# Gram matrix of a 1x1 convolution's input, with the matmul array used in two halves of 64 columns

## The chip, the cores and the metric

One core of a Trainium2 chip runs the whole program in one launch. The metric is device microseconds of one execution, the median of several; lower is better. All data are fp32.

## The reference, cut to what matters

Two ResNet-like bottleneck blocks run one after the other over 64 images of 1024 channels and 14 x 14 pixels (12,544 pixels in all). Batch norm takes its mean and variance from the batch itself.

```python
def block(x, w1, b1, g1, be1, w2, b2, g2, be2, w3, b3, g3, be3, residual_scale):
    out = relu(bn(conv(x, w1, b1, 1, 0), g1, be1))      # 1x1, 1024 -> 256
    out = relu(bn(conv(out, w2, b2, 1, 1), g2, be2))    # 3x3, 256 -> 256
    out = bn(conv(out, w3, b3, 1, 0), g3, be3)          # 1x1, 256 -> 1024
    return relu(x + softplus(residual_scale)[0] * out)
```

The last batch norm needs the mean and variance of the third convolution's output before that output is used. The kernel doesn't compute the output for that. With y the 256-channel input of the third convolution, the mean of y and the Gram matrix G = y y^T / 12,544 are enough: the mean of output channel c is w_c . mean(y), and its mean square is w_c^T G w_c.

## The kernel before, in words

The input of the third convolution stays in SBUF as `y_all`, 128 partitions by two slots of 12,544 pixels: channels on partitions, 256 channels as 2 x 128. A block runs through four stages: the first convolution, the second by a Winograd-like scheme (`conv2`), the Gram stage with the statistics that follow from it (`gram`, `conv3_stats`), and the third convolution with the residual. In block 0 the last is interleaved with the first convolution of block 1 (`fused`); in block 1 it writes the result (`final`).

The change lies in `gram` (line 994) and `conv3_stats` (line 1099), which run once in each block.

**Gram.** The matmul sums over partitions, so pixels must lie on partitions, and y has channels there. Each tile `zt` holds 256 transposed pixels: two chunks (`CH`) of 128 pixels on partitions by 256 channels, and a last column of ones that gives the channel sums along with the products. There are 49 such tiles in a block, made in two ways:

- `by_tensor` (line 1035) makes the first seven: four TensorE transposes of 128 x 128 into PSUM, and a copy by VectorE (DVE) into `zt` (line 1046).
- `by_vector` (line 1049) makes the other 42, in seven steps of six tiles. `spread` (line 1024) first copies 1536 pixels of y by 16 DMAs into a buffer `home` (one of two; in block 0 one of them is the space of `ws`), so that partitions are shuffled in groups of 32. Nine of the 16 are issued by SyncE (SP), seven by GpSimd (POOL). Then DVE transposes 32 x 32 squares (line 1052), one instruction for each tile. The transfer of step k + 2 is issued after step k's transposes, since it takes their buffer. Before it, `norm_to` (line 1012) applies the second batch norm and ReLU to the pixels that it needs: an activation on ScalarE (ACT, line 544) and a subtraction on DVE (`less`, line 1010), which centres y.

Six `zt` buffers (`NZT`) go round. The matmuls of a tile stand one tile behind its making in PE's order (`before` in lines 1087 to 1097). For every 128 pixels there are two: the first 128 channels against all 256 and the ones (257 columns, into PSUM bank `cp`), and the second 128 channels against themselves and the ones (129 columns, into bank `ap`). The block below the diagonal is the mirror of the one above and isn't computed. Orders are written out by hand: instructions wrapped in `tc.keep_in_program_order` keep the order of the program on their engine, the Gram matmuls and transposes among them.

```python
matmul(g0, before[:, c, 0:P], before[:, c, :], start=first, stop=last)
matmul(g1, before[:, c, P:M], before[:, c, P:], start=first, stop=last)
```

After the last tile, `combined` (line 1401) lets DVE make sums of weights for the next stage (lines 148 to 151): eight instructions in block 0, four in block 1.

**Statistics.** `conv3_stats` scales both banks into SBUF by 1 / 12,544: `g0` by DVE (line 1106), `g1` by ACT (line 1107). DVE doubles the off-diagonal block (`off`, line 1108), since it stands for its mirror too. The means are the last columns. DVE multiplies the weights `w3` by them (lines 1116 and 1117). PE then multiplies G with the weights, in two halves of 512 output channels and for each half three matmuls of 512 columns: `t0` from `g0`, `t1` from `off` and then `g1` (lines 1123 to 1125). DVE multiplies `t0` and `t1` by the weights and adds them (lines 1128 and 1129). Two rounds of eight small matmuls with ones (lines 1131 and 1133) sum over partitions and give mean and mean square. From these comes the affine of the last batch norm, and the residual starts.

One product of the third convolution (`conv3`, line 986) stands on PE between the Gram matmuls and the statistics (`made`, line 1409), another right behind them (line 1412).

Of the kernel before, what the change touches and what calls it, by code (L numbers as in the profile page):

```python
# [37 lines left out]
FP = mybir.dt.float32  # L38
AF = mybir.ActivationFunctionType
ALU = mybir.AluOpType  # L40

P = 128
N, C, H, W = 64, 1024, 14, 14
HW = H * W
M = 256
CS = C // P
MS = M // P
# [5 lines left out]
NPX = N * HW  # L53
CH = 2
NZT = 6

FIRST, LAST = 7, 0
RUN = 3 * P
# [29 lines left out]
def bottlenecks(ctx: ExitStack, tc: tile.TileContext, x, w1s, w2s, w3s, pars, out):  # L88
    nc = tc.nc
# [76 lines left out]
    def matmul(*args, **kw):  # L166

        tc.keep_in_program_order(nc.tensor.matmul(*args, **kw))  # L168
# [825 lines left out]
    def gram(psum, pool, homes, aff, minus_c, beside):  # L994

        g0, g1 = psum.tile(M + 1, "cp"), psum.tile(P + 1, "ap")
        zts = [pool.tile([P, CH, M + 1], FP, tag=f"zt{i}", name=f"zt{i}") for i in range(NZT)]
        for zt in zts:  # L1000
            nc.gpsimd.memset(zt[:, :, M:], 1.0)
        zts = itertools.cycle(zts)

        head = 3 * CH * P
        start = FIRST * CH * P
        bounds = [0, CH * P, head, head + STEP, *range(2 * GPX, NPX + 1, GPX)]
        pieces = list(zip(bounds, bounds[1:]))

        def less(s, y):
            tc.keep_in_program_order(nc.vector.tensor_scalar(y, y, minus_c[:, s : s + 1], None, ALU.add))  # L1010

        def norm_to(end):

            while pieces and pieces[0][0] < end:
                a, e = pieces.pop(0)
                for s in reversed(range(MS)):
                    y = y_all[:, s, a:e]
                    if a == 0 and s == 1:
                        norm_vector(s, y, aff, minus_c[:, s : s + 1])
                    else:  # L1020
                        norm(s, y, aff)
                        less(s, y)

        def spread(k):

            first = start + k * STEP if k else head
            norm_to(first + STEP)
            x = homes[k % 2][:, : MS * STEP].rearrange("p (s j f) -> p s j f", s=MS, j=4)
            for i, j in itertools.product(range(4), range(4)):
                queue = nc.gpsimd if 4 * i + j in (1, 3, 6, 8, 10, 13, 15) else nc.sync  # L1030
                a = first + i * RUN
                queue.dma_start(out=x[32 * i : 32 * i + 32, :, j], in_=y_all[32 * j : 32 * j + 32, :, a : a + RUN])
            return x.rearrange("p s j f -> p (s j) f")

        def by_tensor(a):
            tp = psum.tile(CH * M)
            for c in range(CH):
                for s in range(MS):
                    tc.keep_in_program_order(
                        nc.tensor.transpose(  # L1040
                            tp[:, (c * MS + s) * P : (c * MS + s + 1) * P],
                            y_all[:, s, a + c * P : a + (c + 1) * P], ident,
                        )
                    )
            zt = next(zts)
            tc.keep_in_program_order(nc.vector.tensor_copy(zt[:, :, :M], tp.rearrange("p (c m) -> p c m", c=CH)))  # L1046
            return zt

        def by_vector(x, i):
            zt = next(zts)  # L1050
            tc.keep_in_program_order(
                nc.vector.transpose(
                    zt[:, :, :M].rearrange("p b (n c) -> p b n c", c=32),
                    x[:, :, i * CH * 32 : (i + 1) * CH * 32].rearrange("p n (b r) -> p b n r", r=32),
                )
            )
            return zt

        def pairs():

            norm_to(head)
            then = {
                1: lambda: ready.append(spread(0)),
                2: partial(norm_to, 2 * GPX),
                4: partial(norm_to, 3 * GPX),
                5: lambda: ready.append(spread(1)),
            }
            for i in range(FIRST):
# [12 lines left out]
            norm_to(NPX)  # L1081
            for i in range(LAST):
                yield by_tensor(NPX - (LAST - i) * CH * P)

        ready = []
        total = NPX // (CH * P)
        before = None
        for k, zt in enumerate(itertools.chain(pairs(), (None,))):
            if before is not None:
                for c in range(CH):  # L1090
                    first, last = k == 1 and c == 0, k == total and c == CH - 1
                    matmul(g0, before[:, c, 0:P], before[:, c, :], start=first, stop=last)
                    matmul(g1, before[:, c, P:M], before[:, c, P:], start=first, stop=last)
            before = zt
            if k in beside:
                beside[k]()
        return g0, g1

    def conv3_stats(psum, one, grams, w3, mv, tags, spare):


        g0p, g1p = grams
        g0 = one.tile([P, M + 1], FP, tag="g0", name="g0")
        g1 = one.tile([P, P + 1], FP, tag="g1", name="g1")
        off = one.tile([P, P], FP, tag="goff", name="goff")
        nc.vector.tensor_scalar(g0, g0p, 1.0 / NPX, None, ALU.mult)
        nc.scalar.activation(g1, g1p, AF.Copy, scale=1.0 / NPX)
        nc.vector.tensor_scalar(off, g0[:, P:M], 2.0, None, ALU.mult)
        means = g0[:, M:], g1[:, P:]
        wide = 64  # L1110
        sums = [psum.tile(CS * wide, tag).rearrange("p (o k) -> p o k", k=wide) for tag in ("ax", "ap")]
        ones = one.tile([P, 1], FP, tag="ones", name="ones")
        nc.vector.memset(ones, 1.0)
        ones = ones[:, :1].to_broadcast([P, wide])
        by_mean, w = spare[:, :C], [w3[:, s].rearrange("p o c -> p (o c)") for s in range(MS)]
        nc.vector.tensor_scalar(by_mean, w[0], means[0], None, ALU.mult)
        nc.vector.scalar_tensor_tensor(by_mean, w[1], means[1], by_mean, ALU.mult, ALU.add)
        half = CS // 2
        q = one.tile([P, MS, C], FP, tag="q", name="q")
        for h in range(2):  # L1120
            cols = slice(h * half, (h + 1) * half)
            t0, t1 = (psum.tile(half * P, tag) for tag in tags[2 * h : 2 * h + 2])
            matmul(t0, g0[:, 0:P], w3[:, 0, cols, :], start=True, stop=True)
            matmul(t1, off, w3[:, 0, cols, :], start=True, stop=False)
            matmul(t1, g1[:, 0:P], w3[:, 1, cols, :], start=False, stop=True)
            qs = [q[:, s, h * half * P : (h + 1) * half * P] for s in range(MS)]
            for s, t in ((0, t0), (1, t1)):
                nc.vector.tensor_mul(qs[s], t, w3[:, s, cols, :].rearrange("p o c -> p (o c)"))
            nc.vector.tensor_add(qs[0], qs[0], qs[1])
        for o in range(CS):  # L1130
            matmul(sums[0][:, o], by_mean[:, o * P : (o + 1) * P], ones, start=True, stop=True)
        for o in range(CS):
            matmul(sums[1][:, o], q[:, 0, o * P : (o + 1) * P], ones, start=True, stop=True)
        nc.vector.tensor_copy(mv[:, :, 0], sums[0][:, :, 0])
        nc.vector.tensor_copy(mv[:, :, 1], sums[1][:, :, 0])
        sq = small.tile([P, CS], FP, tag="sq", name="sq")
        nc.vector.tensor_mul(sq, mv[:, :, 0], mv[:, :, 0])
        nc.vector.tensor_sub(mv[:, :, 1], mv[:, :, 1], sq)
# [232 lines left out]
    for b in range(2):  # L1371
# [95 lines left out]
```

## Time and profile before

| | us |
|---|---|
| median of 3 runs | 1944.43 (1944.18 to 1944.73) |
| the profiled execution's own time | 1944.06 |
| its span in the trace | 1942.3 |
| PE busy in the span | 1918.6 |
| DVE busy | 1544.3 |
| Gram matmuls of block 0, first start to last end | 589.7 to 659.7 |
| Gram matmuls of block 1, first start to last end | 1555.2 to 1624.7 |
| statistics in block 0 up to the second conv3 product | 659.8 to 669.7 |

PE is TensorE's matmuls and PEld its weight loads, which the profile lists as records of their own. Each fp32 matmul of the program leaves two matmul records and two load records. The starts of matmul records are measured; their ends are modelled, so distances between starts are the prices to read. In a timeline row the columns are the start, the time until the group's end, engine, line, operation, the tiles written and read, the shape, the count, and in brackets the idle time before and what ended it. All matmuls come from one helper and carry its line, L168, so the tile names tell them apart: `cp<-zt` and `ap<-zt` are the Gram matmuls.

### The profile page before, as it was taken

What the parts mean: (1) busy time and instruction counts of PE and PEld (TensorE: products, weight loads), DVE (VectorE), ACT (ScalarE), POOL (GpSimd) and SP (SyncE); (2) the same over time, 40 slices, a digit from 0 to 9 for tenths busy, and PEclk for the clock granted to TensorE, in tenths of its full rate; (3) what the DMA queues carried; (4) which work ended last, traced back from release to release, by engine and by line L of the source; (5) the groups of instructions that cost most, each with busy time, mean ns of one, the idle gap of its engine ahead of it and who ended that gap; (6) DMA issues with size and microseconds to landing.
All of it is one profiled execution on the core that took longest, in us unless ns stands there. A gap on an engine that the chain in (4) does not pass through costs nothing.

```text
span 1942.3 us, 27081 instructions
## 1 busy us (share of the span) xinstructions
PE 1918.6 (99%) x9438; PEld 1612.1 (83%) x9438; DVE 1544.3 (80%) x2473; ACT 1046.2 (54%) x2098; POOL 575.1 (30%) x674
## 2 busy tenths in 40 slices
PE   9999999999999999999999999999999999999999
PEld 5555557999997799999999999989999987555555
DVE  5778667999998667776776767689999975888886
ACT  2222214677765055555555555456777651666666
POOL 0111100212105133433333334302121051666664
PEclk9999999999999999999999999999999999999999
DMA  7777634887948634444444444258788486899998
GB/s 291 273 250 263 235 129 157 204 221 202 230 141 207 197 137 187 175 166 166 181 185 167 166 178 180 108 181 209 215 208 225 140 194 233 279 334 335 333 342 300
DMA packets 201849, 413.91 MB, mean 213 GB/s; under 512 B 37809, under 2 KB 178001, under 8 KB 185201
## 3 DMA queue, kind: packets, MB, share of 16 engines
q1 hardware_dynamic: 161728, 324.66, 49.0%
q0 software_dynamic: 34368, 36.45, 9.3%
q10 hardware_dynamic: 5616, 51.06, 6.3%
q8 instruction: 75, 1.23, 0.3%
q14 instruction: 62, 0.50, 0.1%
HBM read 263.75 MB, written 115.34 MB: 195 GB/s over the span
## 4 chain that ended last, share of the span: by engine, by line
PE 92%; DVE 5%; DMA 1%; ACT 1%; issue 1%; SPq 0%; POOL 0%; DVEq 0%; ACTq 0%
PE cy L168 17%; PE ay L168 17%; PE columns L168 13%; PE cp L168 12%; PE ap L168 10%; PE m L168 6%; PE l L168 6%; PE cx L168 5%; PE ax L168 4%; PE ps L168 1%; DMA home<-y 1%; ACT y L544 1%; DVE v L628 0%; DVE sums L622 0%; DVE steps L697 0%
## 5 line engine op out<-in xcount | busy, mean ns | idle before, releaser
L331 ACT ACTIVATE cu<-cy,scale 128x196 f32<-128x196 f32 (+1 forms) x552 | 256.7, 474 | 277.5 <-PE cy L168 271.3
L168 PE MATMUL columns<-v,ub 128*128 128x224 f32 (+1 forms) x1536 | 300.7, 337 | 0.0
L331 ACT ACTIVATE x<-x,shift 128x392 f32<-128x392 f32 x428 | 241.1, 613 | 59.5 <-POOL x L490 53.1
L168 PEld LDWEIGHTS columns<-v,ub 128*128 128x128 f32 x1536 | 269.2, 188 | 2.8
L464 DVE SCALAR_TENSOR_TENSOR x<-cp,scale,x 128x196 f32<-128x196 f32 (+1 forms) x368 | 178.2, 484 | 97.2 <-PE cp L168 96.1
L168 PE MATMUL cy<-ct,ws 128*128 128x196 f32 (+1 forms) x736 | 221.9, 383 | 1.1 <-ACT cu L331 1.1
L485 POOL TENSOR_TENSOR x<-x,cu 128x196 f32<-128x196 f32 (+1 forms) x184 | 159.3, 866 | 172.1 <-ACT cu L331 162.5
L168 PE MATMUL ay<-at,ws 128*128 128x196 f32 (+1 forms) x752 | 209.1, 381 | 0.0
L490 POOL TENSOR_TENSOR x<-x,cu 128x392 f32<-128x392 f32 x124 | 125.9, 1016 | 192.8 <-DVE x L464 188.1
L168 PEld LDWEIGHTS ay<-at,ws 128*128 128x128 f32 x752 | 136.5, 190 | 33.4
L168 PEld LDWEIGHTS cy<-ct,ws 128*128 128x128 f32 x736 | 133.3, 190 | 36.4 <-ACT cu L331 4.2
L168 PE MATMUL l<-diffs,ub 128*128 128x224 f32 (+1 forms) x768 | 149.1, 337 | 2.6 <-PE columns L168 2.6
L511 POOL TENSOR_TENSOR x<-x,cu 128x392 f32<-128x392 f32 x120 | 121.9, 1017 | 85.9 <-DVE x L464 62.4
L168 PE MATMUL m<-sums,ua 128*128 128x224 f32 (+1 forms) x752 | 145.9, 337 | 1.5 <-DVE sums L622 1.5
L168 PEld LDWEIGHTS l<-diffs,ub 128*128 128x128 f32 x768 | 134.3, 189 | 4.4 <-PE columns L168 3.9
L331 ACT ACTIVATE au<-ay 128x196 f32<-128x196 f32 (+1 forms) x141 | 53.8, 381 | 155.2 <-PE ay L168 152.4
L464 DVE SCALAR_TENSOR_TENSOR x<-cx,scale,x 128x196 f32<-128x196 f32 (+1 forms) x184 | 89.1, 484 | 57.4 <-PE cx L168 57.4
L168 PEld LDWEIGHTS m<-sums,ua 128*128 128x128 f32 x752 | 131.3, 189 | 3.3 <-DVE sums L622 2.9
L168 PE MATMUL cx<-y,w 128*128 128x196 f32 (+1 forms) x404 | 124.1, 392 | 0.4 <-DVE x L1148 0.4
L168 PE MATMUL cy<-y,w 128*128 128x196 f32 (+1 forms) x404 | 123.8, 392 | 0.0
L168 PE MATMUL cp<-zt 128*128 128x257 f32 x392 | 118.0, 382 | 1.8 <-DVE zt L1046 1.7
L168 PE MATMUL cp<-y,ws 128*128 128x196 f32 (+1 forms) x368 | 113.6, 390 | 0.9 <-DVE x L464 0.9
(216 smaller groups left out, 3924.8 us busy)
## 6 DMA issues: line engine op xcount, KB each, us to landing
x<-in_x SPq DMA_DIRECT2D x62, 1568.0 KB, 6.8
ub<-u SPq DMA_DIRECT2D x94, 768.0 KB, 5.2
x<-mid SPq DMA_DIRECT2D x32, 1568.0 KB, 8.2
mid<-x ACTq DMA_DIRECT2D x31, 1568.0 KB, 5.1
out<-x SPq DMA_DIRECT2D x123, 392.0 KB, 5.7
ua<-u SPq DMA_DIRECT2D x94, 256.0 KB, 3.0
u<-y POOLq DMA_DIRECT2D x48, 256.0 KB, 5.8
home<-y SPq DMA_DIRECT2D x90, 96.0 KB, 4.3
```

The costliest lines, as they stand in the source:

```text
L168: tc.keep_in_program_order(nc.tensor.matmul(*args, **kw))
L331: tc.keep_in_program_order(nc.scalar.activation(*args, **kw))
L464: nc.vector.scalar_tensor_tensor(v, bank, self.scale[:, o : o + 1], v, ALU.mult, ALU.add)
L485: nc.gpsimd.tensor_add(self.part(1, 1), self.part(1, 1), u3)
L490: nc.gpsimd.tensor_add(v, v, self.u12)
L511: nc.gpsimd.tensor_add(v, v, self.u12[:, i * self.n : (i + 1) * self.n])
L544: act(y, y, AF.Relu, bias=shift[:, s : s + 1], scale=scale[:, s : s + 1])
```

## The change

The 256 channels are cut into four groups of 64 (`Q`). Of the sixteen 64 x 64 blocks of G ten are computed, each pair of groups once. For every 128 pixels there are four matmuls, each with 64 columns of weights and all 128 rows of the array. A `tile_position` puts them alternately in the array's lower and upper 64 columns, so that their results fall on PSUM partitions 0 to 63 and 64 to 127. Group 0 meets groups 0, 1, 2 and a column of ones (193 columns) and group 1 meets 1, 2, 3 and ones (193), both into bank `cp`; group 2 meets 2, 3 and ones (129), and group 3 meets group 0 with one unused column, then 3 and ones (130), both into bank `ap`. `zt` gets a column of ones at each end, so its channels start at element 1.

In the statistics, five products on DVE with a prepared tile of factors (`by`: once, twice or zero over 12,544) put the blocks into two tiles `g0` and `g1` of 258 columns whose other blocks were zeroed beforehand, and ACT copies one column of means. The off-diagonal factor of two is in the factors. Since blocks of both tiles feed both outputs, each half of the output channels now takes four matmuls of 512 columns: `t0` and `t1` from `g0`, then both from `g1`. On POOL, 13 memsets for `g0`, `g1` and the factors are added at the head of the Gram stage. The order of the other instructions on each engine stays as it was, the transfers on SP and POOL included.

```diff
+Q = P // 2
...
-        g0, g1 = psum.tile(M + 1, "cp"), psum.tile(P + 1, "ap")
-        zts = [pool.tile([P, CH, M + 1], FP, tag=f"zt{i}", name=f"zt{i}") for i in range(NZT)]
+        upper, lower = psum.tile(3 * Q + 1, "cp"), psum.tile(2 * Q + 2, "ap")
+        zts = [pool.tile([P, CH, M + 2], FP, tag=f"zt{i}", name=f"zt{i}") for i in range(NZT)]
         for zt in zts:
-            nc.gpsimd.memset(zt[:, :, M:], 1.0)
+            nc.gpsimd.memset(zt[:, :, 0 : M + 2 : M + 1], 1.0)
...
+        def ends(v):
+            (step, n), (_, _) = v.ap
+            return bass.AP(v.tensor, v.offset + 1, [[step, n], [3 * Q, 2], [1, Q + 1]])
+        by = [pool.tile([P, n], FP, tag=f"by{i}", name=f"by{i}") for i, n in enumerate((3 * Q + 1, 2 * Q + 2))]
+        gs = [pool.tile([P, M + 2], FP, tag=f"g{i}", name=f"g{i}") for i in range(MS)]
+        for g in gs:
+            nc.gpsimd.memset(g, 0.0)
...
+            nc.gpsimd.memset(by[i][here, cols], value)
...
-                    matmul(g0, before[:, c, 0:P], before[:, c, :], start=first, stop=last)
-                    matmul(g1, before[:, c, P:M], before[:, c, P:], start=first, stop=last)
+                    v = before[:, c]
+                    for q, with_ in enumerate((v[:, : 3 * Q + 1], v[:, Q + 1 :], v[:, 2 * Q + 1 :], ends(v))):
+                        here = slice(q % 2 * Q, q % 2 * Q + Q)
+                        to = (upper, lower)[q // 2][here]
+                        to = to[:, : 2 * Q + 1] if q == 2 else to
+                        if q == 3:
+                            to = to.rearrange("p (k m) -> p k m", k=2)
+                        matmul(
+                            to, v[:, 1 + q * Q : 1 + q * Q + Q], with_, start=first, stop=last,
+                            tile_position=(0, q % 2 * Q), skip_group_check=True,
+                        )
...
-        nc.vector.tensor_scalar(g0, g0p, 1.0 / NPX, None, ALU.mult)
-        nc.scalar.activation(g1, g1p, AF.Copy, scale=1.0 / NPX)
-        nc.vector.tensor_scalar(off, g0[:, P:M], 2.0, None, ALU.mult)
-        means = g0[:, M:], g1[:, P:]
+        def scaled(g, a, ps, by):
+            nc.vector.tensor_mul(g[:, a : a + ps.shape[1]], ps, by[:, : ps.shape[1]])
+        scaled(g0[low], 0, upper[low], by[0][low])
+        scaled(g0[high], Q + 1, upper[high], by[0][high])
+        scaled(g1[low], 2 * Q + 1, lower[low, : 2 * Q + 1], by[1][low])
+        n = Q + 1
+        for a, k in (1, 0), (3 * Q + 1, 1):
+            scaled(g1[high], a, lower[high, k * n : k * n + n], by[1][high, k * n : k * n + n])
+        nc.scalar.activation(g0[high, 0:1], g0[high, M + 1 :], AF.Copy)
+        means = g0[:, 0:1], g1[:, M + 1 :]
...
-            matmul(t0, g0[:, 0:P], w3[:, 0, cols, :], start=True, stop=True)
-            matmul(t1, off, w3[:, 0, cols, :], start=True, stop=False)
-            matmul(t1, g1[:, 0:P], w3[:, 1, cols, :], start=False, stop=True)
+            for i, g in enumerate((g0, g1)):
+                for n, t in enumerate((t0, t1)):
+                    matmul(t, g[:, 1 + n * P : 1 + n * P + P], w3[:, i, cols, :], start=i == 0, stop=i == 1)
```

More of the change, by code (lines that the diff above doesn't have):

```diff
@@ L994, in gram @@
     def gram(psum, pool, homes, aff, minus_c, beside):
-        g0, g1 = psum.tile(M + 1, "cp"), psum.tile(P + 1, "ap")
-        zts = [pool.tile([P, CH, M + 1], FP, tag=f"zt{i}", name=f"zt{i}") for i in range(NZT)]
+        upper, lower = psum.tile(3 * Q + 1, "cp"), psum.tile(2 * Q + 2, "ap")
+        zts = [pool.tile([P, CH, M + 2], FP, tag=f"zt{i}", name=f"zt{i}") for i in range(NZT)]
         for zt in zts:
-            nc.gpsimd.memset(zt[:, :, M:], 1.0)
+            nc.gpsimd.memset(zt[:, :, 0 : M + 2 : M + 1], 1.0)
         zts = itertools.cycle(zts)
+        def ends(v):
[3 more added lines that the diff above has]
+        gs = [pool.tile([P, M + 2], FP, tag=f"g{i}", name=f"g{i}") for i in range(MS)]
+        once, twice = 1.0 / NPX, 2.0 / NPX
+        for g in gs:
+            nc.gpsimd.memset(g, 0.0)
+        low, high = slice(0, Q), slice(Q, P)
+        for i, here, cols, value in (
+            (0, low, slice(0, Q + 1), once), (0, low, slice(Q + 1, 3 * Q + 1), twice),
+            (0, high, slice(0, Q), once), (0, high, slice(Q, 3 * Q), twice),
+            (0, high, slice(3 * Q, 3 * Q + 1), once),
+            (1, low, slice(0, Q), once), (1, low, slice(Q, 2 * Q), twice), (1, low, slice(2 * Q, 2 * Q + 1), once),
+            (1, high, slice(0, Q), twice), (1, high, slice(Q, Q + 1), 0.0), (1, high, slice(Q + 1, 2 * Q + 2), once),
+        ):
+            nc.gpsimd.memset(by[i][here, cols], value)
         head = 3 * CH * P
@@ L1045, in by_tensor @@
             zt = next(zts)
-            tc.keep_in_program_order(nc.vector.tensor_copy(zt[:, :, :M], tp.rearrange("p (c m) -> p c m", c=CH)))
+            tc.keep_in_program_order(
+                nc.vector.tensor_copy(zt[:, :, 1 : M + 1], tp.rearrange("p (c m) -> p c m", c=CH))
+            )
             return zt
@@ L1052, in by_vector @@
                 nc.vector.transpose(
-                    zt[:, :, :M].rearrange("p b (n c) -> p b n c", c=32),
+                    zt[:, :, 1 : M + 1].rearrange("p b (n c) -> p b n c", c=32),
                     x[:, :, i * CH * 32 : (i + 1) * CH * 32].rearrange("p n (b r) -> p b n r", r=32),
@@ L1091, in gram @@
                     first, last = k == 1 and c == 0, k == total and c == CH - 1
-                    matmul(g0, before[:, c, 0:P], before[:, c, :], start=first, stop=last)
-                    matmul(g1, before[:, c, P:M], before[:, c, P:], start=first, stop=last)
+                    v = before[:, c]
[8 more added lines that the diff above has]
+                            tile_position=(0, q % 2 * Q), skip_group_check=True,
+                        )
             before = zt
@@ L1096, in gram @@
                 beside[k]()
-        return g0, g1
+        return upper, lower, by, gs
     def conv3_stats(psum, one, grams, w3, mv, tags, spare):
[L1102 to L1105, printed above, removed]
-        nc.vector.tensor_scalar(g0, g0p, 1.0 / NPX, None, ALU.mult)
-        nc.scalar.activation(g1, g1p, AF.Copy, scale=1.0 / NPX)
-        nc.vector.tensor_scalar(off, g0[:, P:M], 2.0, None, ALU.mult)
-        means = g0[:, M:], g1[:, P:]
+        upper, lower, by, (g0, g1) = grams
+        low, high = slice(0, Q), slice(Q, P)
+        def scaled(g, a, ps, by):
[8 more added lines that the diff above has]
+        means = g0[:, 0:1], g1[:, M + 1 :]
         wide = 64
```

## Prediction

> **What bounds the kernel now.** I read the page first (busy shares, then the chain that ended last), then the table of stages, and then the timelines of PE and DVE in the two Gram stages, which the change rewrites (589.7 to 659.7 us in block 0, 1555.2 to 1624.7 in block 1).
>
> ```profile
> PE 1918.6 (99%) x9438; PEld 1612.1 (83%) x9438; DVE 1544.3 (80%) x2473; ACT 1046.2 (54%) x2098; POOL 575.1 (30%) x674
> PE 92%; DVE 5%; DMA 1%; ACT 1%; issue 1%; SPq 0%; POOL 0%; DVEq 0%; ACTq 0%
> 602.60:659.80 57.20, 57.09 (x345) 52.06 (x346) 39.20 (x60) 10.00 (x7) 23.15 (x40) 1.00 0.92 245
> 1568.00:1624.70 56.70, 56.55 (x344) 51.84 (x345) 36.75 (x55) 10.12 (x7) 23.16 (x40) 1.00 0.94 265
> ```
>
> PE is busy throughout, so PE work that goes away counts. But in the last two rows (PE, PEld, DVE, ACT, POOL busy, then clock, DMA share, GB/s) the DMA engines are 92 and 94% busy: a second limit stands close behind PE. The timeline of PE shows the price of 128 pixels:
>
> ```profile
> 608.64 0.60 PE L168 MATMUL cp<-zt 128*128 128x257 f32 x2
> 609.08 0.38 PE L168 MATMUL ap<-zt 128*128 128x129 f32 x2
> 609.30 0.60 PE L168 MATMUL cp<-zt 128*128 128x257 f32 x2
> ...
> 661.94 1.02 PE L168 MATMUL cp<-w,goff 128*128 128x512 f32 x2
> 662.80 1.02 PE L168 MATMUL cp<-w,g 128*128 128x512 f32 x2
> ```
>
> From start to start, 257 columns take 0.44 us, 129 take 0.22, together 0.657 (30.87 us over 47 repeats); 512 take 0.86. One fp32 matmul leaves two records, so a record costs 218.3 ns for 257 columns and 110.7 for 129: that is 0.833 ns a column and 3 to 4 ns more. A tile of 256 pixels costs PE p = 1.316 us. The timeline of DVE tells when tiles arrive:
>
> ```profile
> 611.24 3.68 DVE L1052 STREAM_TRANSPOSE zt<-home 128x512 f32<-128x512 f32 x6 [3.17 <-DMA home<-y]
> 619.48 3.68 DVE L1052 STREAM_TRANSPOSE zt<-ws 128x512 f32<-128x512 f32 x6 [2.69 <-DMA home<-y]
> 625.43 3.71 DVE L1052 STREAM_TRANSPOSE zt<-home 128x512 f32<-128x512 f32 x6 [0.41 <-DMA ws<-y]
> 633.83 3.68 DVE L1052 STREAM_TRANSPOSE zt<-ws 128x512 f32<-128x512 f32 x6 [2.61 <-DMA home<-y]
> 639.64 2.65 DVE L1052 STREAM_TRANSPOSE zt<-home 128x512 f32<-128x512 f32 x4 [2.14 <-DMA ws<-y]
> ...
> 647.33 1.90 DVE L1052 STREAM_TRANSPOSE zt<-ws 128x512 f32<-128x512 f32 x3 [2.42 <-DMA ws<-y]
> ```
>
> Every step of six tiles begins when its transfer lands, not when PE asks. A step's transfer starts after the transposes of the step two before it, which also waited on a transfer; PE holds DVE back only from 642.9 on (zt buffers). So these landings stay where they are however fast PE is.
>
> **What the Trainium skill says.** (1) "FP8 and Floating Point Precision", TensorE Precision Notes: true fp32 is four passes through the array. The trace agrees: 4 x 257 / 2.4 = 428 ns against 0.44 us. (2) "TensorE: Matmul & The Clock Gate", Part 3: matmuls in different column groups run at once (three of 32 columns, 2.38 times), and Part 2: matmuls keep program order. No run here shows column groups, nor what fp32's two records do in them. (3) The same page, Part 2, LDWEIGHTS: time goes with the columns, P / 1.2. For 128 that is 107 ns; the 64-column sums, bound by it, come every 112 ns in the trace (x15 in 1.75 us, less one load's 0.19, is 14 intervals). Loads of 64 columns are not in the trace; my estimate from the page is 53. (4) "TensorEngine Tiling (Array Packing)", Key Properties: changing the mode drains TensorE. Not in the trace.
>
> **The change, part by part.**
>
> *Gram matmuls.* Per 128 pixels, 257 + 129 columns go; 193, 193, 129 and 130 come, each with 64 weight columns, alternately in the low and high half. Run one after another they would be 645 columns instead of 386. I need the overlap. Call the records (193 columns: a = 161 ns; 130: d = 108) A.hi, A.lo, B.hi, B.lo, C.hi, C.lo, D.hi, D.lo, A and C low, B and D high. Kept in program order, B.hi cannot start before A.lo, which waits for A.hi in its own half. So neighbours across instructions overlap, not whole pairs: A.lo with B.hi, B.lo with C.hi, C.lo with D.hi (which must wait for B.lo), D.lo with the next A.hi. Starts: A.hi at 0, A.lo and B.hi at a, B.lo and C.hi at 2a, D.hi at 3a, D.lo and the next A.hi at 3a + d = 591 ns. With 4 ns for each of four such transitions, 607 ns: p = 1.213. Bounds: both halves fully independent, 323 columns x 4 / 2.4 + 16 = 555, p = 1.11; no overlap, 1075 + 8 x 4 = 1107, p = 2.21. Eight 64-column loads at 57 ns (53 and the trace's 4) are 456 ns and hide under 607.
>
> *What of it reaches the end.* PE ends the stage at the latest of T + 0.73 + 6 n p over the steps, T a step's landing, n the steps from it to the last, 0.73 the first transpose and its signal. Check with p = 1.316 in block 0: the step at 619.48, n = 5, gives 659.7, as in the trace. With 1.213: 619.48 gives 656.6, 633.83 (n = 3) 656.4, 647.33 (n = 1) 655.3: end 656.6, gain 3.1. In block 1 the trace's landings are 1576.02, 1582.54, 1590.84, 1597.52, 1604.06, 1611.65; the tile at 1568.15 and its 42 followers give 1624.7 for 1.316 (trace 1624.7); with 1.213, 1590.84 (n = 4) gives 1620.7: gain 4.1. Sum 7.2 us, where 98 x 2 x 51 ns would be 10: the rest turns into waits for transfers.
>
> *After the Gram.* The off-diagonal blocks now need both g tiles for both outputs: four 512-column matmuls per half instead of three, two more per block, 4 x 0.86 = +3.4 us. PE runs without a gap from 661.1 to 669.7 there, so all of it counts.
>
> *Scaling.* DVE's 257-column scaling (0.43), the doubling (0.23) and ACT's copy give way to five products of 64 partitions, 193, 193, 129, 65, 65 elements, and ACT's copy of one column. Nearest price: 0.69 us for 512 from PSUM; 0.16 + N / 960 us gives 0.36, 0.36, 0.29, 0.23, 0.23. The first two, 0.7 us, release the first matmul; the other conv3 product (ay, 1.32 us on PE) covers them: nothing. Without that cover, 0.7 a block. Behind the five on DVE wait the products with the means, 0.4 us later, under 3.4 us of matmuls; behind ACT's copy nothing waits for 10 us.
>
> *Other edits.* Thirteen more memsets on POOL (0.1 us each by the zt row, perhaps 0.3) come before its first transfer issue, whose wait for y ends at 592.98, 8.6 us after the last memset: nothing; they would cost only past that. zt written one element further along: no cost seen between its two halves today, one of which already starts on an odd element. Mode changes between transposes and Gram at the stage's start: two lie on the chain that issues the second transfer (595.1 to 596.9), I take 0.15 us each block, 0 to 0.4.
>
> *Sum* against the profiled execution, 1944.06 us: - 7.2 + 3.4 + 0.3 = 1940.6. The median of the runs is 0.37 higher: 1941.0.
>
> **Rivals.**
> 1. *Full overlap*, p = 1.11. For: equal lengths in a pair, independent halves. Against: hi and lo of one matmul are consecutive. Block 1 gains 6.5 (last landing 1611.0, since step 4's transposes wait less, + 0.73 + 6.7 = 1618.4). Block 0 would end at 654.7, but DVE then still builds weight sums (5.15 us, begun when its transposes end, about 651.0, so to 656.2); PE restarts at about 657.3, gain 3.8. -10.3 + 3.4 + 0.3: 1937.9.
> 2. *The slower side: no overlap.* Place: the Gram matmuls; PE takes the two halves in turn, because their passes or loads exclude each other. p = 2.21, 0.894 more a tile: the last 43 tiles then run unbroken and add some 38.2 a block (602.63 + 43 x 2.21 = 697.7 in block 0, against 659.7), the first six 5.4 less the 2.3 us that PE idles there (10.65 busy of 12.9), 3.1. 2 x 41.3 + 3.7: 2030.7. For: nothing in the trace has ever shown two PE records at once; the skill says a load overlaps a running matmul only in another row group, and these share all rows (though the trace hides full loads under matmuls today). Against: the column packing that the skill measured. It decides from p = 1.265 on (632 ns per 128 pixels), where the formula gains just 3.7.
> 3. *Loads bound it.* If 64 columns load as slowly as 128 (112 ns), 8 x 112 = 896 ns, p = 1.8: by the same count 2 x (20.6 + 0.6) + 3.7: 1990.5. If loads are only half hidden, something between.
> 4. *The transfers slow down*: the landing chain does not depend on PE, so I give it no separate time.
>
> **How the numbers follow.** Staggered overlap 38%, 1941.0 (1939 to 1942.5); full overlap 22%, 1937.9 (to 1937); loads or part of the overlap lost 20%, 1943 to 1991; no overlap 20%, 2030.7. The range 1937 to 1991 leaves out the last. About 0.2% (3.9 us) is what measurement can tell from no change. Faster by more: full overlap and a third of the staggered, 0.35; within: the other two thirds and little of the third case, 0.28; slower: 0.37. The likeliest signs are mixed; its own range is 1939 to 1942.5.
>
> **What would show it.** Right: records of zt matmuls in the two halves overlapping, a period near 607 ns per 128 pixels, DVE's landings unmoved, DVE's waits on ap at the last steps gone, PE waiting for zt before the last steps, four 512-column products per half. Wrong: a period near 1107 (no overlap), 896 (loads) or 555 (independent halves), or later landings.

## The result, and the profile after

The changed kernel takes 1940.03 us (median of 12 runs, 1938.35 to 1943.8), the kernel before 1944.42 on the same chip (12 runs, 1943.52 to 1944.73). The ratio is 0.9979, with a 95% interval of 0.9971 to 0.9987: a gain of 4.4 us. The profiled execution took 1940.31 us with a span of 1938.5. From the page, engines and chain:

```profile
PE 1905.8 (98%) x10230; PEld 1595.8 (82%) x10230; DVE 1543.5 (80%) x2479; ACT 1046.2 (54%) x2098; POOL 578.5 (30%) x700
PE 83%; DVE 6%; issue 5%; DMA 3%; ACT 1%; POOL 1%; SPq 1%; DVEq 0%; POOLq 0%; ACTq 0%
```

PE has 792 records more and is busy 12.8 us less. The chain that ended last was 92% PE before and is 83% now. Of the 9 points, 4 went to "issue", time for which the profile shows no wait, 2 to transfers, and one each to DVE, POOL and the issuing on SP. The timeline of PE in the Gram stage shows the overlap:

```profile
608.76 0.50 PE L170 MATMUL cp<-zt 128*64 128x193 f32 x4
609.09 0.40 PE L170 MATMUL ap<-zt 128*64 128x129 f32 x4
609.31 0.50 PE L170 MATMUL cp<-zt 128*64 128x193 f32 x4
```

The period of 128 pixels, 608.76 to 609.31, is 0.549 us when measured over many repeats; before it was 0.657. Four records of 193 columns span 0.50 us. Two behind one another would span 0.161 + 0.326 = 0.49 (161 ns to the next, 326 for the last as modelled); three staggered steps would give 0.65. So the low and the high half each take two, at the same time. The tile view gives the durations (shortest, median, longest in ns):

```profile
L170 PEld LDWEIGHTS cp<-zt x784: 132/135/138, 590.1 to 1618.0; 128*64 128x64 f32 x196
L170 PE MATMUL cp<-zt x784: 324/326/380, 590.1 to 1618.1; 128*64 128x193 f32 x196
```

The timeline of DVE in block 0 shows where the time went that PE no longer needs:

```profile
611.40 3.68 DVE L1077 STREAM_TRANSPOSE zt<-home 128x512 f32<-128x512 f32 x6 [2.45 <-DMA home<-y]
619.11 3.68 DVE L1077 STREAM_TRANSPOSE zt<-ws 128x512 f32<-128x512 f32 x6 [2.17 <-DMA home<-y]
625.86 3.68 DVE L1077 STREAM_TRANSPOSE zt<-home 128x512 f32<-128x512 f32 x6 [1.21 <-DMA ws<-y]
633.88 3.68 DVE L1077 STREAM_TRANSPOSE zt<-ws 128x512 f32<-128x512 f32 x6 [2.28 <-DMA home<-y]
639.34 3.68 DVE L1077 STREAM_TRANSPOSE zt<-home 128x512 f32<-128x512 f32 x6 [1.78 <-PE ap L170]
647.78 3.68 DVE L1077 STREAM_TRANSPOSE zt<-ws 128x512 f32<-128x512 f32 x6 [4.76 <-DMA ws<-y]
```

All six tiles of each step now run in one piece: in the kernel before the last two steps broke up (x4, x3) because PE had not given zt back. What is left are waits for pixels; the last is 4.76 us long. (The releaser at 639.34 is put down to ap, which had long been done: the other thing waited for is the transfer.) The end of that chain, from the chain of waits:

```profile
633.89 3.68 DVE zt L1077 x6
637.59 0.59 SPq L1055
...
643.18 0.59 SPq L1055
643.82 3.55 DMA ws<-y
648.42 3.05 DVE zt L1077 x5
651.49 0.70 DVE ws L150
```

Transposes free a buffer, nine issues on SP and a transfer follow, then transposes and DVE's weight sums; PE isn't in it. At its end, from the timelines of DVE and of PE:

```profile
655.96 0.68 DVE L153 TENSOR_TENSOR ws<-w,ws 128x512 f32<-128x512 f32 x1
656.56 0.74 DVE L1140 TENSOR_TENSOR g<-cp,by 64x193 f32<-64x193 f32 x2
657.33 0.69 DVE L1140 TENSOR_TENSOR g<-ap,by 64x129 f32<-64x129 f32 x3
```

```profile
655.28 1.58 PE L170 MATMUL ay<-y,w 128*128 128x392 f32 x4
657.35 1.12 PE L170 MATMUL cy<-w,g 128*128 128x512 f32 x2 [0.49 <-DVE g L1140]
658.32 1.02 PE L170 MATMUL cp<-w,g 128*128 128x512 f32 x2
...
663.47 1.02 PE L170 MATMUL cx<-w,g 128*128 128x512 f32 x2
```

The eight weight sums end last, so PE waits 0.49 us for the scaling; then come eight matmuls of 512 columns instead of six. The stage in numbers, from one trace of each kernel (block 0 / block 1, us). The start is the first transpose on PE. The last landing is taken as the start of the last step's transposes, counted from there; without transfers nothing lands and PE sets it. The last three rows are kernels of the next section.

| kernel | last landing | start to first product with g | from there to the start of the sums' last matmul |
|---|---|---|---|
| before | 59.55 / 58.34 | 73.30 / 72.76 | 8.56 / 8.56 |
| after | 59.54 / 60.10 | 69.11 / 69.03 | 10.38 / 10.27 |
| mixed pair | 59.49 / 58.43 | 69.07 / 68.01 | 9.01 / 8.90 |
| after, no transfers | 51.78 / 51.54 | 65.16 / 64.92 | 10.27 / 10.27 |
| after, half runs | 53.12 / 54.56 | 64.96 / 65.86 | 10.27 / 10.27 |

Gram: -4.19 - 3.73 = -7.9. Statistics: +1.82 + 1.71 = +3.5. Together -4.4, the difference of the medians. The two profiled spans differ by 3.8: the rest of the program took 0.6 us more in the profile of after, spread over stages that the change doesn't touch.

### The profile page after: what moved, and what is told of

Same layout as the page of the kernel before. It is cut to its first block, busy times and chain, and to the rows that moved or that the text cites. A ratio compares the mean times of both kernels' runs of the same rounds, so it can differ in the third digit from the quotient of the medians.

```text
span 1938.5 us, 28704 instructions
## 1 busy us (share of the span) xinstructions
PE 1905.8 (98%) x10230; PEld 1595.8 (82%) x10230; DVE 1543.5 (80%) x2479; ACT 1046.2 (54%) x2098; POOL 578.5 (30%) x700
## 4 chain that ended last, share of the span: by engine, by line
PE 83%; DVE 6%; issue 5%; DMA 3%; ACT 1%; POOL 1%; SPq 1%; DVEq 0%; POOLq 0%; ACTq 0%
PE cy L170 17%; PE ay L170 14%; PE columns L170 13%; PE cp L170 9%; PE ap L170 7%; PE m L170 6%; PE l L170 6%; PE cx L170 5%; PE ax L170 4%; DMA home<-y 2%; DVE zt L1077 1%; PE ps L170 1%; SPq L1055 1%; ACT y L546 1%; POOL u L217 1%
## 5 line engine op out<-in xcount | busy, mean ns | idle before, releaser
L874 POOL DMA_DIRECT2D y<-f x24 | 30.8, 1521 | 274.1 <-DVE f L800 272.1
```

What stands on the lines that cost most here:

```text
L874: nc.gpsimd.dma_start(out=out_rows[3][:, o], in_=fa[:, o, :full], accum_op=ALU.add)
```

## The experiments

The kernel before was timed again beside each group of runs: 1944.06 to 1944.21 us there, 1944.42 beside the changed kernel.

**Order of the four matmuls.** Low, low, high, high: in the staggered model, which keeps program order, neighbours run together only where the half changes.

```diff
-                    for q, with_ in enumerate((v[:, : 3 * Q + 1], v[:, Q + 1 :], v[:, 2 * Q + 1 :], ends(v))):
+                    four = list(enumerate((v[:, : 3 * Q + 1], v[:, Q + 1 :], v[:, 2 * Q + 1 :], ends(v))))
+                    for q, with_ in [four[i] for i in (0, 2, 1, 3)]:
```

> Same four Gram matmuls, issued in the order low 193, low 129, high 193, high 130. Theory A (each half of the array has a queue of its own and looks several matmuls ahead): period per 128 pixels stays at 549 ns and the time within 1 us of the changed kernel's 1940. Theory B (the other half's next matmul starts early only when it directly follows in the program): low 129 runs with high 193, high 130 with the next low 193, so the period is 2 x 193 columns, about 650 ns, and the time about 1948. Strict program order of starts over both halves (the prediction's staggered model): 4 x 161 + 2 x 108 = 860 ns, about 1990.

Measured: 1938.94 us (one run), a period of 548 ns. From the timeline of PE in this kernel:

```profile
625.62 0.55 PE L170 MATMUL cp<-zt 128*64 128x193 f32 x4
625.95 0.44 PE L170 MATMUL ap<-zt 128*64 128x129 f32 x4
626.17 0.55 PE L170 MATMUL cp<-zt 128*64 128x193 f32 x4
```

The same groups and the same period as in the changed kernel, from another program order. Program order doesn't bind across the halves at this distance.

**Unequal lengths side by side.** The order 0, 3, 2, 1 in the same line puts 193 columns beside 130 and 129 beside 193.

> Order low 193, high 130, low 129, high 193: unequal lengths beside each other, the same sum in each half. Theory A (independent queues): 549 ns again, no change of time. Theory B (a pair starts together and waits for its longer member): 193 + 193 columns, about 650 ns a period, 1948.

Measured: 1939.86 us (one run), a period of about 549 ns. Equal lengths side by side, which the prediction counted in favour of a full overlap, aren't needed where the two halves have the same sum (323 and 322 columns). Halves with unequal sums were not run.

**How far PE looks ahead.** Two probes give one half a longer run of work before the other gets any. In the first all four matmuls of a chunk of 128 pixels go to one half; in the second all eight of a tile. The sums that they form are not those of the Gram matrix.

```diff
-                        here = slice(q % 2 * Q, q % 2 * Q + Q)
+                        here = slice(c * Q, c * Q + Q)
...
-                            tile_position=(0, q % 2 * Q), skip_group_check=True,
+                            tile_position=(0, c * Q), skip_group_check=True,
```

> All four matmuls of an even chunk go to the low half, all four of an odd chunk to the high half (their sums fall over one another, so the Gram matrix is not the wanted one; the work is the same). The other half's work now stands four matmuls, eight records, away. Theory A with a look ahead of at least eight matmul records: 549 ns per 128 pixels on average, 1940. With a shorter look ahead, one half mostly waits for the other: up to 1107 ns per 128 pixels, 2031, which is also the price of no overlap.

> As the run by chunk, but the half changes with the tile of 256 pixels: eight matmuls, 16 records, go to one half before the other has its turn (the sums again fall over one another). Theory from the 548 ns of the order low low high high and the 712 ns of the run by chunk: a half can start a record only while it stands at most four to five matmul records behind the oldest one that still runs. Replayed with such a window, 880 to 936 ns per 128 pixels, about 1990 us. If the look ahead were of some other kind [...], 549 ns or the 712 of before.

Measured: 1960.68 and 1997.94 us (one run each); 712 and 904 ns per 128 pixels. From the timelines of PE, first by chunk, then by tile:

```profile
625.01 0.49 PE L170 MATMUL cp<-zt 128*64 128x193 f32 x2
625.34 0.27 PE L170 MATMUL ap<-zt 128*64 128x129 f32 x1
625.34 0.38 PE L170 MATMUL cp<-zt 128*64 128x193 f32 x1
```

```profile
621.33 0.60 PE L170 MATMUL ap<-zt 128*64 128x129 f32 x4
621.78 0.82 PE L170 MATMUL cp<-zt 128*64 128x193 f32 x4
622.43 0.27 PE L170 MATMUL ap<-zt 128*64 128x129 f32 x1
622.43 0.38 PE L170 MATMUL cp<-zt 128*64 128x193 f32 x1
```

At 625.34 and 622.43 a matmul of the next run starts in one half while the last ones of the earlier run (129 or 130 columns) still go in the other. Before that PE works on one half alone: the four cp records from 621.78 take 0.82 us, one behind another, where the changed kernel's four take 0.50. So the overlap has a reach. Suppose that the two records of a matmul follow each other, that a record may start only among the first W records counted from the oldest one still running, and that its own half must be free. Replaying the trace's distances between starts under this assumption gives these ns per 128 pixels:

| W | after | low, low, high, high | half by chunk | half by tile |
|---|---|---|---|---|
| 2 (the prediction's staggered model) | 605 | 880 | 991 | 1047 |
| 3 | 552 | 657 | 879 | 991 |
| 4 | 552 | 552 | 768 | 936 |
| 5 | 552 | 552 | 657 | 880 |
| 6 | 552 | 552 | 551 | 798 |
| measured | 549 | 548 | 712 | 904 |

The first two columns need three and four records or more; the two probes lie between the values for four and for five (the second was forecast so, at 880 to 936). No single W gives all four, so some four to five records is a fit; what inside PE does it was not shown.

**The transfers away.** Both kernels without the transfers of steps 2 to 6 (the buffers keep older pixels), so that DVE never waits for them.

```diff
-            for i, j in itertools.product(range(4), range(4)):
+            for i, j in itertools.product(range(4), range(4)) if k < 2 else ():
```

> The kernel before with the transfers of steps 2 to 6 left out in both Gram stages: the tiles are made again from the pixels of steps 0 and 1, so the Gram matrix is of other pixels. Theory (before, PE was the limit and the transfers only just kept up): 43 tiles x 1.316 us unbroken, 0.5 us less in block 0 and nothing in block 1, 1943.7. Rival (transfers already cost much): several us less.

> The changed kernel with the same transfers left out. Theory (the landings now set the end of the Gram stages): PE runs unbroken, 43 x 1.10 us from the eighth tile on; block 1 ends 5.4 us earlier, block 0 gains only some 2.6 since DVE's eight sums of weights then end last: about 1932. Rival (PE's own pace or DVE's transposes set the end): no change, 1940. Theory also expects that the runs spread less than those of the changed kernel (1938.35 to 1943.8).

Measured: the kernel before 1944.94 us (1944.18 to 1946.11), a ratio to itself with transfers of 1.0005 [0.9997, 1.0013]; the changed kernel 1932.08 us (1931.27 to 1933.47), 0.994 [0.9926, 0.9953]. The kernel before gains nothing (0.5 us was expected): there PE was the bound and the landings had slack. The changed kernel gains 8 us, and DVE then waits on PE for each tile (timeline of DVE, changed kernel without transfers):

```profile
632.81 0.71 DVE L1077 STREAM_TRANSPOSE zt<-home 128x512 f32<-128x512 f32 x1 [0.38 <-PE ap L170]
633.91 0.71 DVE L1077 STREAM_TRANSPOSE zt<-home 128x512 f32<-128x512 f32 x1 [0.39 <-PE ap L170]
635.01 0.71 DVE L1077 STREAM_TRANSPOSE zt<-home 128x512 f32<-128x512 f32 x1 [0.39 <-PE ap L170]
```

A tile comes every 1.097 us, which is p. With pixels at hand the change is worth 12.9 us (1944.94 to 1932.08); with transfers 4.4. The spread of the runs settles nothing: it is 5.5 us in 12 runs of the changed kernel and 2.2 in 4 runs without transfers, but in the kernel before it is 1.2 in 12 runs with them and 1.9 in 12 without.

**What in the transfers?** The chain above runs through a buffer becoming free, nine issues on SP and a transfer. Four kernels were made to separate these. Three start from the "mixed pair" kernel described last in this section (1936.86 us). First, a third buffer, so that steps don't wait for transposes:

```diff
-            x = homes[k % 2][:, : MS * STEP].rearrange("p (s j f) -> p s j f", s=MS, j=4)
+            x = homes[k % 3][:, : MS * STEP].rearrange("p (s j f) -> p s j f", s=MS, j=4)
...
-                if k + 2 < STEPS:
-                    ready.append(spread(k + 2))
+                    if k == 0 and i == 2:
+                        ready.append(spread(2))
+                if k + 3 < STEPS:
+                    ready.append(spread(k + 3))
```

> The version with the taken-back statistics matmuls, and a third home buffer: the transfer of step k + 3 is issued after step k's transposes, and that of step 2 after the third transpose of step 0. If the transfers are late because each waits for its buffer: landings some 2 us earlier at the last step, 1933 to 1935. If the DMA engines are simply full (92 to 94% busy): landings as before, 1936 to 1937.

Measured: 1938.3 us (1937.31 to 1940.43), 0.9972 [0.996, 0.9984]: no gain. More buffers alone don't help. But the timeline of SP's queue in this kernel shows that SP now issues almost without a pause, 7 to 8 us a step:

```profile
600.89 14.45 SPq L1055 DMA_DIRECT2D home<-y  x18
615.44 7.90 SPq L1055 DMA_DIRECT2D ws<-y  x9
623.46 13.89 SPq L1055 DMA_DIRECT2D home<-y  x18
```

So a rival stays: with free buffers, SP's issuing could be what holds this kernel back. No run has the third buffer and a lighter SP together. Second, five of SP's nine issues moved to ACT:

```diff
-                queue = nc.gpsimd if 4 * i + j in (1, 3, 6, 8, 10, 13, 15) else nc.sync
+                queue = nc.gpsimd if 4 * i + j in (1, 3, 6, 8, 10, 13, 15) else nc.scalar if k > 1 and j % 2 == 0 else nc.sync
```

> The version with the taken-back statistics matmuls; from step 2 on ACT issues five of SP's nine transfers, so the longest queue has seven issues of 0.6 us in place of nine of 0.7. If the pace of issuing makes the landings late: last landing 1.5 to 2 us earlier in each block, 1933.5 to 1935. If the DMA engines are full: landings and time as before, 1936 to 1937.

Measured: 1956.93 us (1954.94 to 1957.62), 1.0062 [1.0045, 1.0079]. The expectations missed: with SP's queue shorter, the scheduler moved the next stage's loads of x forward, in between the steps. From the timeline of SP's queue:

```profile
608.49 4.95 SPq L1055 DMA_DIRECT2D ws<-y  x4
613.57 0.50 SPq L125 DMA_DIRECT2D x<-in_x  x1
615.49 12.34 SPq L1055 DMA_DIRECT2D home<-y  x4
```

Each is 1.57 MB, as much as a whole step. The last landings came at 67.4 and 70.3 us after the stage's start, not at 59.5 and 58.4, and the 7.9 and 12.1 us by which the first product with g comes later are the 20 us that this kernel lost. It doesn't separate issuing from bytes as it was meant to. Third, eight issues on each queue instead of nine and seven, with SP's order otherwise untouched:

```diff
-                queue = nc.gpsimd if 4 * i + j in (1, 3, 6, 8, 10, 13, 15) else nc.sync
+                queue = nc.gpsimd if 4 * i + j in (1, 3, 4, 6, 8, 10, 13, 15) else nc.sync
```

> The version with the two statistics matmuls taken back (1936.86 us), with the transfers of a step shared out as eight on GpSimd's queue and eight on SyncE's, where they were seven and nine. If the pace of issuing on SyncE (nine a step at some 0.7 us each) sets when a step's pixels land, each landing comes some 0.7 us earlier, and over the three transfers that are chained one behind another in a stage about 2 us a block: 1933 to 1935 us. If the DMA engines are full in these stages, the split of the issuing doesn't matter: 1936 to 1937.5 us.

Measured: 1940.83 us (1938.78 to 1941.87), 0.9981 [0.9973, 0.999]. Neither expectation holds: SP finishes its issues sooner, and the time is 4 us longer. The table of stages in block 0 (us busy of PE, PEld, DVE, ACT, POOL, then clock, DMA share, GB/s), for the mixed pair, then the even split, then the third buffer:

```profile
602.60:645.00 42.40, 38.62 (x550) 34.97 (x552) 29.68 (x45) 11.32 (x9) 23.10 (x39) 1.00 0.93 216
```

```profile
602.60:645.00 42.40, 36.71 (x516) 32.42 (x514) 29.02 (x44) 11.11 (x8) 27.60 (x47) 1.00 1.02 209
```

```profile
602.60:645.00 42.40, 37.32 (x508) 34.05 (x506) 28.85 (x44) 13.34 (x10) 24.77 (x41) 0.96 1.02 221
```

(The clock of 0.96 in the third buffer's line is a stretch of 3.41 us at half the granted clock, after PE had idled for 3.78 us. It ends 20 us before the last step begins, and DVE waits for pixels three times in between.)

The DMA share goes from 0.93 to 1.02 (it adds up the times of all packets, so it can pass 1), and the rate stays at 209 to 221 GB/s. In block 1, from 1566 to 1608 us, the three kernels have shares of 0.82, 1.00 and 1.04 and 215, 210 and 227 GB/s. A share higher by up to 27% thus goes with a rate higher by 6% at most: the requests mainly take longer. So the engines look full at the mixed pair's shares already, which the fourth kernel tests on the changed kernel itself: the same issues and the same number of runs, half the bytes.

```diff
-                queue.dma_start(out=x[32 * i : 32 * i + 32, :, j], in_=y_all[32 * j : 32 * j + 32, :, a : a + RUN])
+                part = slice(0, RUN if k < 2 else RUN // 2)
+                queue.dma_start(out=x[32 * i : 32 * i + 32, :, j, part], in_=y_all[32 * j : 32 * j + 32, :, a : a + RUN][:, :, part])
```

> The changed kernel (1940.03 us), with each transfer of steps 2 to 6 of a stage cut to 192 of its 384 pixels a run (the other pixels stay those of an older step, so the Gram matrix is not the wanted one); the same sixteen issues on the same queues, the same number of runs, half the bytes. If the bytes that the DMA engines move in these stages set the landings, they come early, as in the kernel without these transfers (1932.08 us): 1932 to 1935. If issuing, the latency of a transfer or a cost per run sets them, they stay: 1939 to 1941.

Measured: 1934.13 us (1931.94 to 1935.44), 0.9947 [0.9931, 0.9964]. The table of stages of this kernel, and its DMA issues (KB each, median us from issue to landing):

```profile
602.60:645.00 42.40, 41.27 (x599) 39.94 (x601) 33.36 (x52) 9.93 (x7) 24.06 (x40) 1.00 0.65 164
```

```profile
ws<-y SPq DMA_DIRECT2D x27, 48.0 KB, 2.1
ws<-y POOLq DMA_DIRECT2D x21, 48.0 KB, 2.3
```

The same lines of the changed kernel have 96.0 KB and 4.9 and 4.7 us. With SP still issuing nine a step, the last landings come 6.4 and 5.5 us earlier. So the bytes set the landings in the changed kernel; a fixed cost of an issue, of a transfer or of a run doesn't. Issuing is the next limit, and it is close. Here SP issues almost without a pause, 6.0 to 6.7 us a step. In block 0 of the changed kernel a step takes some 7.3 us, and SP issues for 6.2 to 7.4 us in each.

The Trainium skill, "DMA: Bandwidth & Descriptors", Where 436 GB/s comes from, says that for copies from SBUF to SBUF the fabric's 435 GB/s bind. These copies come nowhere near it: at DMA shares of 0.82 to 1.04 the stretches above move 209 to 227 GB/s, about half, and the measurement decides. Why half, no run here shows.

**The statistics matmuls taken back.** With two halves, a product with one 64-row block of g can run beside another. Block (3,0) goes into the unused corner of the first g tile, ACT makes a mixed copy of the weights, and two pairs of 64 columns side by side replace four full matmuls: six times 0.86 us instead of eight.

```diff
+        mixed = spare[:, C : 2 * C].rearrange("p (o c) -> p o c", c=P)
+        for i, part in enumerate((low, high)):
+            nc.scalar.activation(mixed[part], w3[part, i], AF.Copy)
...
+        def beside(h):
+            for i, (part, v) in enumerate(((low, mixed), (high, w3[:, 0]))):
+                matmul(
+                    banks[2 * h][part], g0[:, 1 + i * Q : 1 + i * Q + Q], v[:, halves[h], :], start=True, stop=True,
+                    tile_position=(0, i * Q), skip_group_check=True,
+                )
```

> The extra 512-column matmuls of the statistics are taken back: the block of groups 3 and 0 is put into the unused corner of g0, and t0 is made by two 64-column matmuls beside each other, the lower one with a copy of the weights whose lower partitions hold slot 0 and upper partitions slot 1 (made by ACT early). Theory: the extra matmuls lie wholly on the path, so 2 x 1.72 us less, plus 0.3 us a block for changing the mode twice: 1937.2. Rival: DVE's products behind them are the path, then little or nothing comes back, 1940.

Measured: 1936.86 us (1934.24 to 1938.07), 0.9962 [0.9948, 0.9975], the fastest version with the whole computation: 7.3 us below the kernel before on its chip (1944.12). From its timeline of PE:

```profile
657.70 0.64 PE L170 MATMUL cy<-home,g 128*64 128x512 f32 x1
657.71 0.64 PE L170 MATMUL cy<-w,g 128*64 128x512 f32 x1
658.18 0.59 PE L170 MATMUL cy<-home,g 128*64 128x512 f32 x1
658.18 0.59 PE L170 MATMUL cy<-w,g 128*64 128x512 f32 x1
```

Two records start within 10 ns of each other, and between its changes of mode a pair takes the 0.43 us of a single one (from 658.18 to the next pair at 658.61). The statistics take 9.01 and 8.90 us against 10.38 and 10.27: 1.37 less in each block. Two matmuls fewer would be 1.72, so going to the halves and back costs 0.35.

## Why the prediction was right, and where it was wrong

The time (1941.0 forecast, 1940.03 measured) and the signs of its two main terms hold, but that the time came so close is partly luck: two errors cancelled. PE overlaps more than forecast, and pixels landed later in block 1 than forecast.

1. **The failed step: "Kept in program order, B.hi cannot start before A.lo".** It can. From the start times of single records in the changed kernel (ns from the first, at 620.64 us):

   | A.lo, B.lo | C.hi, D.hi | C.lo, D.lo | next A.hi, B.hi | next A.lo |
   |---|---|---|---|---|
   | 0, 5 | 162, 167 | 272, 280 | 381, 391 | 544 |

   B.hi starts 10 ns after A.hi and 153 ns before A.lo, which stands ahead of it. (The trace doesn't name halves or passes; that a matmul's two records follow each other is the prediction's reading.) So the 607 ns forecast for 128 pixels are 549, p is 1.098 and not 1.213: rival 1's full overlap, which got 22%. Its 555 ns also follow from the trace before: 323 columns in two records at 0.833 ns, and 16 ns for four starts, are 554. The order low, low, high, high confirms it without that reading, and the probes put the reach at some four to five records. The prediction relied on the Trainium skill's "TensorE: Matmul & The Clock Gate", which keeps matmuls strictly in program order, in Part 2 and again in Part 3, What overlaps and what doesn't; across column halves this trace shows otherwise. "TensorEngine Tiling (Array Packing)", Key Properties, says that different tiles can load and multiply in parallel, and with that the trace agrees.

2. **The formula for the end holds.** Landing + 0.73 + 6 n p, with 1.098 and after's own last landings (n = 1): 59.54 + 0.73 + 6.6 = 66.9 in block 0, 60.10 + 7.3 = 67.4 in block 1; the last Gram records start at 66.83 and 67.40. It was p that was wrong, and now the last step decides, so that the end hangs on p only six times and not 43.

3. **That "these landings stay where they are" holds on average only.** Block 0's last landing is unmoved (59.54 against 59.55). Block 1's came 1.8 us later. Rival 1 had counted on 0.65 earlier. In four kernels with this Gram and all their transfers unchanged (the changed one, the two other orders, the mixed pair), the last landings lie between 58.3 and 60.1 with a mean of 59.1, beside 58.95 before. So the mean stays, the scatter is some 1 us, and the end of the Gram stage now follows it. This is the mis-sized term of rival 1, whose 1937.9 would otherwise have been the better number: 57.7 + 7.3 would end the Gram 2.4 us earlier in block 1. With the landings of before, the measured p would have gained 4.2 and 5.5 us (an estimate from the table and the formula of point 2), 9.7 together: the greater overlap is worth 2.5 us more than the forecast 7.2, and the later landing takes 1.8 of them back. That the gross gain of 7.9 is near the forecast is this offset. (Rival 1's own sum has a slip: from its 1618.4 and 1624.7 block 1 gains 6.3, not 6.5, which makes it 1938.0.)

4. **The second limit was named rightly, but sized too small.** The DMA engines at 92 and 94% were "a second limit" that "stands close behind PE". The prediction let waits for transfers take 2.8 us (10 less 7.2). Without transfers the Gram stages would have gained 8.1 and 7.8 us, not 4.19 and 3.73, so they take some 8. That the bytes set it, the half runs show; a third buffer or a shorter queue on SP alone gained nothing, and the kernel with ACT says nothing on it. Why the even split of issues costs 4 us at the same bytes is open: its steps take about 7.6 us instead of 7.2, and nothing here separates more requests in flight from the queue they come from.

5. **Statistics: +3.4 forecast, +3.5 measured.** All of it counts, as forecast: PE runs there without a gap. The mixed pair takes 2.7 back.

6. **Scaling.** The cover given for block 0 ("the other conv3 product (ay, 1.32 us on PE) covers them: nothing") fails, as rival 1 foresaw: DVE's weight sums end at 656.6 and PE waits 0.49 us. In block 1 the sums end earlier and the scaling waits 1.28 us for PE. The five products take 0.74 + 0.69 us; 1.47 was forecast.

7. **Mode changes: the net is as forecast, the gross is not.** The prediction took 0.15 us a block for two changes on the chain to the second transfer, and that chain is 0.15 and 0.16 us longer (9.87 and 9.88 against 9.72 from the stage's start). But a tile with its four transposes takes PE 1.83 us (1.75 before). Two chunks at 0.549 and the transposes at 0.44 would be 1.54, so two changes cost 0.29, and the shorter Gram matmuls hide most of it. The same working for before, two chunks at 0.657 and 0.44, gives its 1.75. The mixed pair's 0.35 for two more changes is of the same size.

8. **Memsets on POOL: nothing**, as forecast. The thirteen take 1.9 us, and POOL's first transfer still waits 6.79 us for y.

The rivals of no overlap (1107 ns) and of loads as the bound (896) are out. The load records of 64 columns are 135 ns long against 190 for 128, and eight of them disappear under 549 ns.

## What to carry to other kernels

In these kernels fp32 matmuls in two column halves of PE run fully beside each other in each of the three program orders tried, as long as the other half's next work lies within a few records. Pairs need not have equal lengths when the halves have equal sums. When PE stands near a second limit, price the change with the second limit removed and with it in place (here 12.9 and 4.4 us), since what is left depends on that limit and not on the overlap alone. And where an engine seems to wait on issuing, halve the bytes at the same issues before moving the issues.

## What the runs showed of the hardware that was not expected

- PE starts records of the free half up to some four or five records ahead (549, 548, 712 and 904 ns in four arrangements).
- Sixteen copies a step from SBUF to SBUF in runs of 1.5 KB stay at 209 to 227 GB/s. A third buffer or an even split of the issues raised the DMA share from 0.93 to 1.02 (0.82 to 1.04 in block 1), and the rate by 6% at most.
- One issue more on POOL and one fewer on SP in each step cost 4 us, with the order on SP otherwise unchanged.
- Long waits of PE came with half the granted clock: for 3.41 us at the end of idle stretches of 3.78 us (third buffer) and 2.84 us (ACT issuing), and for 6.83 us from within idle stretches of 7.35 and 8.18 us (ACT issuing). 128 pixels then take 1.07 us instead of 0.55 (third buffer). A wait of 1.99 us was followed by 3.41 us of it (low, low, high, high), one of 1.97 us was not (unequal lengths). The profile of the changed kernel has none of it in these stages: PE's longest idle stretch there is 1.63 us.
